# Tying each instruction to the one ahead of it on its engine, and placing every writer of a reused tile behind the old tile's readers

## The chip, the cores and the metric

One core of one Trainium2 chip. The metric is the device time of one execution in microseconds (us), on the slowest (here the only) core. "PE" is TensorE, "PEld" its weight load, "DVE" VectorE, "ACT" ScalarE, "POOL" GpSimd, "SP" SyncE. SBUF and PSUM are the on-chip memories that the kernel's tiles lie in (its matmuls write to banks of PSUM); a semaphore is a counter by which one engine waits for another. All timed runs below are of the fast state; in none did the granted TensorE clock averaged over the run fall under 0.988.

## The reference

Four graph layers on 128 graphs of 64 nodes with 256 features, each followed by a residual and a layer norm. Cut to what matters:

```python
x = layernorm(x + gated(x, adj))         # 5 rounds: message product, sum over neighbours, GRU cell
x = layernorm(x + mlp(adj @ x))          # 256 -> 1024, RMS norm, SiLU, 1024 -> 256
x = layernorm(x + hyperbolic(adj @ x))   # artanh (a logarithm), then tanh and a projection
x = layernorm(x + attention(x, adj))     # softmax-like weights by exp, masked by adj
```

## The kernel before

The graphs are worked on in 16 groups of 8. The kernel does not write its instructions straight out. It records every operation with an engine, an assumed duration, what it reads and what it writes; a beam search (one that carries several unfinished plans along and keeps the best) then simulates the engines and looks for an order in which PE never waits; the operations are emitted in the order found, which is called the plan below. Groups overlap, so that while one group waits for a small chain on DVE or ACT, PE works for another.

```python
    def op(self, eng, us, run, w=(), r=(), kb=0):          # record one operation
        ...
        for accesses, writes in ((r, False), (w, True)):
            for a in accesses:
                b, part = a if isinstance(a, tuple) else (a, None)
                if not b.uses and b.slot is not None:       # first use of a buffer in a reused slot:
                    ring = self.slots.setdefault(b.slot[0], deque(maxlen=b.slot[1]))
                    if len(ring) == b.slot[1]:
                        before.update(u[0] for u in ring[0].uses)   # behind all uses of the old one
                    ring.append(b)
        ...

    WINDOW, STRETCH, WIDTH, LAG = 4, 25.0, 8, 40.0          # groups looked at, us per decision, plans kept

    def issue(self):
        ...                                                 # the beam search
        for part in reversed(parts):
            for o in part:
                o.run()                                     # emit, in the plan's order
```

Below this lies a second scheduler, that of the framework. It takes the emitted instructions with their data dependencies, puts them in an order of its own on each engine, and adds the semaphores. Emission order is only a hint to it.

The operations that the argument comes back to:

```python
# a gated layer: copy of a partial product out of PSUM; the next product goes into the same bank after it
act(420, lambda: nc.scalar.copy(uu.tile(), blocks_of(p1.tile())), [uu], [p1])
...
# second layer: residual plus bias, added on GpSimd from two SBUF tiles
pool(2.35, lambda: nc.gpsimd.tensor_tensor(xb.tile(), x1.tile(), over(b2_r.tile(), NB), OP.add), [xb], [x1, b2_r])
...
# third layer: the logarithm of artanh, on ACT, with a table load before it and another after it
act(2600, lambda: nc.scalar.activation(fac.tile(), fac.tile(), AF.Ln), [fac], [fac])
...
# set-up: small vectors spread to all partitions by GpSimd's queue; sums over a_r on DVE into junk_d
a_r = everywhere(a_w, 2 * D, "a_r")
```

Of the kernel before, what the change touches and what calls it, by code (L numbers as in the profile page):

```python
# [14 lines left out]
OP = mybir.AluOpType  # L15
# [4 lines left out]
MIN_NORM = 1e-15  # L20
MAX_ARG = float(np.float32(1 - 1e-7))
MAX_NORM = 1.0 - 0.004
SERIES_BELOW = 0.25
# [3 lines left out]
class Buf:  # L27


    def __init__(self, make, slot=None, bank=False):  # L30
        self.make, self.slot, self.bank = make, slot, bank
        self.ap, self.uses, self.left = None, [], 0

    def __getitem__(self, i):
        return self.tile()[i]
# [15 lines left out]
class Plan:  # L51


    def __init__(self, flow):
# [4 lines left out]
        self.uses = {}  # L59
        self.clock = dict.fromkeys(flow.AHEAD, 0.75)  # L60
        self.queues = [{e: deque(o for o in s if o.eng == e) for e in self.clock} for s in flow.streams]
# [15 lines left out]
    def advance(self, until, rank):  # L77
# [3 lines left out]
        while self.left and clock["PE"] < until:  # L81
            best = None
            for s in range(self.first, min(self.first + flow.WINDOW, len(self.queues))):
                for e, q in self.queues[s].items():
                    opened = False
                    for _, o in zip(range(flow.AHEAD[e]), q):
                        t = max(clock[e], at[o.id])
# [53 lines left out]
class Flow:  # L141
# [7 lines left out]



    AHEAD = {"PE": 32, "DVE": 10, "ACT": 10, "POOL": 4, "SP": 2}

    HOPS = {"from PE": 0.25, "to PE": 0.3, "else": 0.1}
# [3 lines left out]
    TRANSFERS = 8  # L158
    WINDOW, STRETCH, WIDTH, LAG = 4, 25.0, 8, 40.0

    def __init__(self):
        self.streams, self.slots = [], {}

    def stream(self):
        self.ops = []
# [2 lines left out]
    def op(self, eng, us, run, w=(), r=(), kb=0):  # L168
        o = Op(eng, us, run, len(self.streams) - 1, len(self.ops), kb)
        before = set()  # L170
# [3 lines that stand above are left out]
                if not b.uses and b.slot is not None:  # L174
                    ring = self.slots.setdefault(b.slot[0], deque(maxlen=b.slot[1]))
                    if len(ring) == b.slot[1]:
                        before.update(u[0] for u in ring[0].uses)
                    ring.append(b)
                for u, p, wr in b.uses:
                    if (wr or writes) and (p is None or part is None or p == part):  # L180
                        before.add(u)
        before.discard(o)
        touched = set()
# [3 lines that stand above are left out]
                if b.bank and not b.uses:  # L187
                    o.opens = b
                b.uses.append((o, part, writes))
                if b not in touched:  # L190
                    touched.add(b)
                    b.left += 1
        o.bufs = [b for b in touched if b.bank]
        o.need = len(before)
        for u in before:
            u.then.append(o)
        self.ops.append(o)
# [18 lines left out]
    def issue(self):  # L216
        self.ways()
        ranks = (lambda s, o: (s, o.n), lambda s, o: (s if o.kb else -s, o.n), lambda s, o: (self.LAG * s - o.way, s, o.n))
        plans, until = [Plan(self)], 0.0
        while any(p.left for p in plans):  # L220
            until += self.STRETCH
            found = {}
            for p in plans:
                for rank in ranks:
                    c = p.copy()
                    if c.advance(until, rank):
                        found.setdefault((round(c.bound(), 3), c.left), c)
            plans = [found[k] for k in sorted(found)[:self.WIDTH]]
        p, parts = plans[0], []
        past = (p.past, p.order)  # L230
        while past is not None:
            parts.append(past[1])
            past = past[0]
        for part in reversed(parts):
            for o in part:
                o.run()


@with_exitstack
def kernel(  # L240
# [31 lines left out]
    nc = tc.nc  # L272
# [7 lines left out]
    KD = D // P  # L280
# [8 lines left out]
    small = ctx.enter_context(tc.tile_pool(name="small", bufs=2))  # L289
    psum = ctx.enter_context(tc.tile_pool(name="psum", bufs=BANKS, space=bass.MemoryType.PSUM))  # L290

    flow = Flow()
    quads = [slice(t * N, (t + 1) * N) for t in range(2)]


    def fixed(shape, name):
        return Buf(lambda: const.tile(shape, F32, name=name))
# [11 lines left out]


    def matmul(o, lhsT, rhs, k, nk):
        nc.tensor.matmul(o, lhsT, rhs, start=(k == 0), stop=(k == nk - 1))  # L312

    def pe(n, run, w, r):
        flow.op("PE", {512: 0.86, 256: 0.435, 257: 0.44, 128: 0.23}.get(n, 0.3), run, w, r)
# [4 lines left out]
    def dve(n, run, w, r):  # L320
        flow.op("DVE", 0.16 + 0.00105 * n, run, w, r)
# [44 lines left out]
    one4 = const.tile([P, NB], F32, name="one4")  # L366
# [28 lines left out]
    NV = 3 * KD  # L395
    NC = 2 * NV + 2 * KH
    cols = fixed([P, NC], "cols")
    half_b = fixed([P, NV], "half_b")
# [53 lines left out]


    def halves():
        nc.vector.tensor_add(half_b[:, :2 * KD], cols[:, :2 * KD], cols[:, NV:NV + 2 * KD])
        nc.vector.tensor_copy(half_b[:, 2 * KD:], cols[:, NV + 2 * KD:2 * NV])
        nc.vector.tensor_scalar(half_b.tile(), half_b.tile(), 0.5, None, OP.mult)
    dve(300, halves, [half_b], [cols])

    def turned(src, nf, out_of):  # L460
# [97 lines left out]
    def group(g):  # L558
        s = g % NF

        def tiny(name, shape=(P, NB), dt=F32):
            t = f"{name}{s}"
            return Buf(lambda: small.tile(list(shape), dt, tag=t, name=f"{name}_{g}"), slot=(t, 2))

        def u(tag, name, shape=(P, R)):
            return unit(tag, s, f"{name}_{g}", shape, bufs(tag))
# [27 lines left out]
        def aggregate(dst, src, b0, n):  # L594

            ps = bank("ps_agg")
            for j in range(2):
                for c in range(KD):
                    pe(128, lambda j=j, c=c: matmul(
                        ps[:, c * HR + j * P:c * HR + (j + 1) * P], src[:, b0 + j, c * P:(c + 1) * P],  # L600
                        ed[:, 2 * n + j, :], 0, 1), [ps], [(src, b0 + j), ed])
            act(512, lambda: nc.scalar.copy(dst[:, :, half(n)], blocks_of(ps.tile())), [(dst, n)], [ps])  # L602
            return ps
# [49 lines left out]
        for t in range(2):  # L653
            q = quads[t]
# [123 lines left out]
        for n in range(2):  # L778
            ps = rows_of(hT, n)
            for j in range(2):  # L780
                b = 2 * n + j
# [5 lines left out]
        for t in range(2):  # L787
            q = quads[t]
# [40 lines left out]
        for c in range(KH):  # L829
# [4 lines left out]
            th = u("VZR"[c % 3], f"th{c}")  # L834
# [5 lines left out]
        for h in range(NB // 2):  # L840
            ps = bank("ps_o1")
            for j in range(2):
                b = 2 * h + j
# [4 lines left out]
            for j in range(2):  # L848
                b = 2 * h + j
                dve(256, lambda ps=ps, b=b, j=j: nc.vector.scalar_tensor_tensor(  # L850
                    y1[:, b, :], ps[:, j * D:(j + 1) * D], 0.5, xb[:, b, :], OP.mult, OP.add), [(y1, b)], [ps, (xb, b)])
        xn = tiny("n")
# [3 lines left out]
        rn, fac, n2, ser = (tiny(t) for t in ("rn", "fac", "n2", "ser"))  # L856
        near = tiny("near", dt=I32)
# [9 lines left out]


        def series():
            nc.vector.tensor_mul(n2.tile(), xn.tile(), xn.tile())  # L870
            nc.vector.scalar_tensor_tensor(ser.tile(), n2.tile(), 1.0 / 13.0, one4, OP.mult, OP.mult)
            for q in (11, 9, 7, 5, 3):
                nc.vector.scalar_tensor_tensor(ser.tile(), ser.tile(), 1.0 / q, n2.tile(), OP.add, OP.mult)
            nc.vector.tensor_add(ser.tile(), ser.tile(), one4)
            nc.vector.scalar_tensor_tensor(near.tile(), xn.tile(), SERIES_BELOW, one4, OP.is_lt, OP.mult)
        dve(1250, series, [n2, ser, near], [xn])
        dve(4, lambda: nc.vector.scalar_tensor_tensor(fac.tile(), fac.tile(), 0.5, rn.tile(), OP.mult, OP.mult),
            [fac], [fac, rn])
# [7 lines left out]
        for h in range(NB // 2):  # L886
            for j in range(2):
                b = 2 * h + j
                pe(256, lambda b=b, j=j, ps=sup[h]: matmul(
                    ps[:, j * D:(j + 1) * D], adjT[:, b, :], tan[:, b, :], 0, 1), [sup[h]], [adjT, (tan, b)])  # L890
            for j in range(2):
                b = 2 * h + j
# [3 lines left out]
        un, unb, th, urn = tiny("n"), tiny("n2"), tiny("th"), tiny("rn")  # L896
# [3 lines left out]


        def onto_ball():
            nc.vector.tensor_mul(th.tile(), th.tile(), urn.tile())
            nc.vector.tensor_mul(un.tile(), th.tile(), un.tile())
            nc.vector.scalar_tensor_tensor(un.tile(), un.tile(), MIN_NORM, un.tile(), OP.max, OP.max)  # L905
            nc.vector.reciprocal(un.tile(), un.tile())
            nc.vector.scalar_tensor_tensor(un.tile(), un.tile(), MAX_NORM, one4, OP.mult, OP.min)
            nc.vector.tensor_mul(th.tile(), th.tile(), un.tile())
        dve(4, lambda: nc.vector.reciprocal(urn.tile(), unb.tile()), [urn], [unb])
        dve(800, onto_ball, [th, un], [th, un, urn])  # L910
        y2 = rows("y", "y2")
        for b in range(NB):
# [22 lines left out]
        for t in range(2):  # L935
            q = quads[t]
# [5 lines left out]
        for t in range(2):  # L942
            q = quads[t]
# [11 lines left out]
        o = layer_norm(y3, "A", "n3")  # L955
# [38 lines left out]
```

## Time and profile before

| | before |
|---|---|
| time, median of 4 | 2511.1 us (2510.5 to 2511.9) |
| span of the profiled run | 2509.0 us |
| PE busy / idle | 2438.9 / 70.1 us |
| DVE, ACT busy | 66%, 47% |
| sum of all PE instructions at their spacing | 2409 us |

The lines themselves are in the prediction. A row of the stretches gives start and end, the length, then for PE, PEld, DVE, ACT and POOL the busy time with the number of records, then granted clock, DMA share and GB/s. In a line of the timeline the first two numbers are start and duration; square brackets hold the engine's idle time just before, and what ended it.

One more measure is used throughout. PE's order of work is known from the program, and each PE instruction has a spacing when nothing holds it (0.432 us for 256 columns, and so on, as the prediction lists them). I add up these spacings along PE's order and call the running sum **PE work**, from 0 to 2409 us. A **gap** is what the distance between two starts has beyond the spacing. Gaps sorted by PE work can be compared between kernels of different length. For the kernel before: 10.1 us in the first 60 us of PE work (the start), 43.3 from 60 to 2100 (the middle), 3.9 from 2100 to 2330, and 30.6 beyond (the end).

### The profile page before, as it was taken

The numbers are of one execution on the slowest core, as the hardware profiler recorded it, in microseconds if no ns is written. First come the engines' busy times: TensorE is split into PE (matmuls) and PEld (weight loads), VectorE is DVE, ScalarE is ACT, GpSimd is POOL, SyncE is SP. The second block draws the span as 40 slices with busy tenths as digits, with TensorE's granted clock in tenths as the row PEclk, the third lists the DMA queues.
The fourth block names the chain that finished last, engine by engine and source line by source line (L and its number), as shares of the span: only waits on it lengthen the run. The fifth ranks groups of instructions, "written<-read, shape, count | busy, mean of one in ns | idle before, by whom it ended". The sixth has DMA issues, their size and how long they took to land. (4 is left out here: it accounts for less than half of the span.)

```text
span 2509.0 us, 31864 instructions
## 1 busy us (share of the span) xinstructions
PE 2438.9 (97%) x11986; PEld 2047.4 (82%) x11986; DVE 1659.8 (66%) x3725; ACT 1188.6 (47%) x2500; POOL 179.1 (7%) x146
## 2 busy tenths in 40 slices
PE   8999999999999999999999999999999999999995
PEld 6887887888787887887878878887888887878874
DVE  2656677667577676666776766676766665666766
ACT  3444445445445445445454454455445445444643
POOL 4001000000001000000010000010000000000011
PEclk9999999999999999999999999999999999999998
DMA  4000000000000000000000000000000000000000
GB/s 125 1 1 9 1 9 20 1 9 28 1 20 9 20 9 20 1 19 9 1 28 1 20 9 1 9 28 1 20 28 1 11 18 1 9 20 9 1 9 26
DMA packets 39146, 35.12 MB, mean 14 GB/s; under 512 B 9892, under 2 KB 38592, under 8 KB 38992
## 3 DMA queue, kind: packets, MB, share of 16 engines
q1 hardware_dynamic: 37264, 31.20, 3.9%
q8 instruction: 95, 1.56, 0.3%
q10 hardware_dynamic: 1328, 1.31, 0.2%
q0 software_dynamic: 400, 0.57, 0.1%
q14 instruction: 59, 0.48, 0.1%
HBM read 24.69 MB, written 8.39 MB: 13 GB/s over the span
## 5 line engine op out<-in xcount | busy, mean ns | idle before, releaser
L609 PE MATMUL p_hn<-hT,w_hn 128*128 128x256 f32 x1280 | 320.7, 380 | 0.0
L609 PE MATMUL p_in<-agg,w_in 128*128 128x256 f32 x1280 | 311.9, 379 | 0.0
L609 PEld LDWEIGHTS p_in<-agg,w_in 128*128 128x128 f32 x1280 | 241.3, 190 | 32.6 <-issue 1.0
L609 PEld LDWEIGHTS p_hn<-hT,w_hn 128*128 128x128 f32 x1280 | 229.0, 191 | 29.4 <-issue 4.8
L312 PE MATMUL ps_o<-w2s,hid 128*128 128x256 f32 x1024 | 234.0, 381 | 3.4 <-DVE n L905 3.0
L312 PE MATMUL ps_hid<-aggm,w1s 128*128 128x512 f32 x512 | 229.0, 592 | 0.0
L312 PEld LDWEIGHTS ps_o<-w2s,hid 128*128 128x128 f32 x1024 | 193.2, 191 | 30.2 <-issue 3.2
L624 POOL TENSOR_TENSOR rstd<-ve,pow 128x4 f32<-128x4 f32 (+1 forms) x64 | 77.5, 1211 | 1823.6 <-DVE ve L622 1823.5
L713 ACT ACTIVATE V<-V,half_b 128x256 f32<-128x256 f32 x160 | 72.8, 500 | 267.9 <-DVE V L709 267.9
L312 PEld LDWEIGHTS ps_hid<-aggm,w1s 128*128 128x128 f32 x512 | 95.3, 190 | 97.1 <-issue 92.4
L609 PE MATMUL p_r<-hT,a 128*128 128x256 f32 x640 | 155.1, 380 | 7.2 <-ACT U L739 5.9
L609 PE MATMUL p_u<-tA,s 128*128 128x256 f32 x640 | 157.3, 384 | 4.9 <-DVE tA L692 2.3
L609 PE MATMUL p_w<-tA,s 128*128 128x256 f32 x640 | 160.2, 380 | 1.7 <-DVE tA L692 1.7
L609 PE MATMUL p_r<-agg,a 128*128 128x256 f32 x640 | 153.4, 380 | 5.9 <-ACT agg L602 4.9
L609 PE MATMUL p_v<-tB,s 128*128 128x256 f32 x640 | 156.7, 379 | 0.0
L678 ACT ACTIVATE hnb<-p_hn,half_b 128x256 f32<-128x256 f32 x320 | 135.5, 471 | 44.6 <-PE p_hn L609 42.4
L609 PE MATMUL p_v<-tB,na 128*128 128x256 f32 x640 | 153.8, 380 | 2.1 <-DVE V L709 2.0
L722 DVE SCALAR_TENSOR_TENSOR R<-R,hnb 128x512 f32<-128x512 f32 x80 | 56.1, 701 | 150.1 <-ACT R L713 150.0
L609 PE MATMUL p_w<-hT,s 128*128 128x256 f32 x640 | 155.4, 379 | 0.0
L602 ACT COPY agg<-ps_agg 128x512 f32<-128x512 f32 x160 | 93.0, 583 | 119.2 <-PE ps_agg L312 94.4
L312 PEld LDWEIGHTS ps_agg<-edge,hr 128*128 128x128 f32 x1024 | 134.6, 191 | 11.3 <-ACT hr L672 4.9
L609 PEld LDWEIGHTS p_r<-hT,a 128*128 128x128 f32 x640 | 120.2, 190 | 28.4 <-ACT U L739 7.9
(206 smaller groups left out, 4447.1 us busy)
## 6 DMA issues: line engine op xcount, KB each, us to landing
x<-in_x_dram SPq DMA_DIRECT2D x16, 512.0 KB, 3.8
xr<-in_x_dram SPq DMA_DIRECT2D x16, 512.0 KB, 3.5
out_dram<-x_n SPq DMA_DIRECT2D x16, 512.0 KB, 2.8
edge<-in_adj_dram SPq DMA_DIRECT2D x32, 64.0 KB, 2.3
wm<-in_L_gnn_weight_dram SPq DMA_DIRECT2D x5, 256.0 KB, 7.3
w1s<-in_L_gnn_W_dram SPq DMA_DIRECT2D x1, 1024.0 KB, 6.8
w2s<-in_L_gnn_W_dram SPq DMA_DIRECT2D x1, 1024.0 KB, 9.6
aw_in_L_gnn_w_hh_dram<-in_L_gnn_w_hh_dram ACTq DMA_DIRECT2D x1, 512.0 KB, 5.3
```

What stands on the lines that cost most here:

```text
L312: nc.tensor.matmul(o, lhsT, rhs, start=(k == 0), stop=(k == nk - 1))
L602: act(512, lambda: nc.scalar.copy(dst[:, :, half(n)], blocks_of(ps.tile())), [(dst, n)], [ps])
L609: pe(256, lambda c=c, k=k: nc.tensor.matmul(ps[:, c * HR:(c + 1) * HR], w[:, k, c * P:(c + 1) * P], v(k), start=first and c == k == 0, sto ...
L624: pool(1.1, lambda: nc.gpsimd.tensor_tensor(rstd[:, :m, :], ve[:, :m, :], pow2[:, :m, :], OP.pow), [rstd], [ve])
L678: act(300, lambda c=c: nc.scalar.activation(hnb[:, c, half(n)], p_hn[:, c * HR:(c + 1) * HR], AF.Identity, bias=half_b[:, 2 * KD + c:2 * K ...
L713: act(256, lambda c=c: nc.scalar.activation(o[:, c, :], src(c), AF.Tanh, bias=half_b[:, i * KD + c:i * KD + c + 1], scale=0.5), [(o, c)], ...
L722: dve(512, lambda: nc.vector.scalar_tensor_tensor(t.tile(), t.tile(), 1.0, hnb[:, :, half(n)], OP.add, OP.mult), [t], [t, (hnb, (n, 0)), ( ...
```

## The change

Its intent: the search's order is to reach the chip. Every emitted instruction gets an ordering edge, without a semaphore, to the one emitted before it on its engine (the "ties"). And where a slot is reused, not the first writer alone but each writer is planned behind the old tile's uses (the "writers"). The helpers now return their instructions so that the ties can be drawn; those lines are cut.

```diff
@@ Flow
+    BEHIND = mybir.DependencyInfo(mybir.DependencyClass.NoSync, mybir.DependencyReason.DATA)
...
                     if len(ring) == b.slot[1]:
-                        before.update(u[0] for u in ring[0].uses)
+                        b.after = {u[0] for u in ring[0].uses}
                     ring.append(b)
+                if writes:
+                    before.update(b.after)
...
+        last = {}
         for part in reversed(parts):
             for o in part:
-                o.run()
+                made = o.run()
+                for i in made if isinstance(made, list) else [made]:
+                    if o.eng in last:
+                        self.tc.add_manual_dep(i.ins, last[o.eng].ins.name, self.BEHIND, reason="the plan's order")
+                    last[o.eng] = i
```

More of the change, by code (lines that the diff above doesn't have):

```diff
@@ L31, in __init__ @@
         self.make, self.slot, self.bank = make, slot, bank
-        self.ap, self.uses, self.left = None, [], 0
+        self.ap, self.uses, self.left, self.after = None, [], 0, ()
     def __getitem__(self, i):
@@ L159, with __init__ @@
     WINDOW, STRETCH, WIDTH, LAG = 4, 25.0, 8, 40.0
-    def __init__(self):
-        self.streams, self.slots = [], {}
+    BEHIND = mybir.DependencyInfo(mybir.DependencyClass.NoSync, mybir.DependencyReason.DATA)
+    def __init__(self, tc):
+        self.tc, self.streams, self.slots = tc, [], {}
     def stream(self):
@@ L290 @@
     psum = ctx.enter_context(tc.tile_pool(name="psum", bufs=BANKS, space=bass.MemoryType.PSUM))
-    flow = Flow()
+    flow = Flow(tc)
     quads = [slice(t * N, (t + 1) * N) for t in range(2)]
@@ L311, in matmul @@
     def matmul(o, lhsT, rhs, k, nk):
-        nc.tensor.matmul(o, lhsT, rhs, start=(k == 0), stop=(k == nk - 1))
+        return nc.tensor.matmul(o, lhsT, rhs, start=(k == 0), stop=(k == nk - 1))
     def pe(n, run, w, r):
@@ L454, in halves @@
     def halves():
-        nc.vector.tensor_add(half_b[:, :2 * KD], cols[:, :2 * KD], cols[:, NV:NV + 2 * KD])
-        nc.vector.tensor_copy(half_b[:, 2 * KD:], cols[:, NV + 2 * KD:2 * NV])
-        nc.vector.tensor_scalar(half_b.tile(), half_b.tile(), 0.5, None, OP.mult)
+        return [nc.vector.tensor_add(half_b[:, :2 * KD], cols[:, :2 * KD], cols[:, NV:NV + 2 * KD]),
+                nc.vector.tensor_copy(half_b[:, 2 * KD:], cols[:, NV + 2 * KD:2 * NV]),
+                nc.vector.tensor_scalar(half_b.tile(), half_b.tile(), 0.5, None, OP.mult)]
     dve(300, halves, [half_b], [cols])
@@ L869, in series @@
         def series():
-            nc.vector.tensor_mul(n2.tile(), xn.tile(), xn.tile())
-            nc.vector.scalar_tensor_tensor(ser.tile(), n2.tile(), 1.0 / 13.0, one4, OP.mult, OP.mult)
-            for q in (11, 9, 7, 5, 3):
-                nc.vector.scalar_tensor_tensor(ser.tile(), ser.tile(), 1.0 / q, n2.tile(), OP.add, OP.mult)
-            nc.vector.tensor_add(ser.tile(), ser.tile(), one4)
-            nc.vector.scalar_tensor_tensor(near.tile(), xn.tile(), SERIES_BELOW, one4, OP.is_lt, OP.mult)
+            v = nc.vector
+            return [
+                v.tensor_mul(n2.tile(), xn.tile(), xn.tile()),
+                v.scalar_tensor_tensor(ser.tile(), n2.tile(), 1.0 / 13.0, one4, OP.mult, OP.mult),
+                *(v.scalar_tensor_tensor(ser.tile(), ser.tile(), 1.0 / q, n2.tile(), OP.add, OP.mult)
+                  for q in (11, 9, 7, 5, 3)),
+                v.tensor_add(ser.tile(), ser.tile(), one4),
+                v.scalar_tensor_tensor(near.tile(), xn.tile(), SERIES_BELOW, one4, OP.is_lt, OP.mult)]
         dve(1250, series, [n2, ser, near], [xn])
@@ L902, in onto_ball @@
         def onto_ball():
-            nc.vector.tensor_mul(th.tile(), th.tile(), urn.tile())
-            nc.vector.tensor_mul(un.tile(), th.tile(), un.tile())
-            nc.vector.scalar_tensor_tensor(un.tile(), un.tile(), MIN_NORM, un.tile(), OP.max, OP.max)
-            nc.vector.reciprocal(un.tile(), un.tile())
-            nc.vector.scalar_tensor_tensor(un.tile(), un.tile(), MAX_NORM, one4, OP.mult, OP.min)
-            nc.vector.tensor_mul(th.tile(), th.tile(), un.tile())
+            v = nc.vector
+            return [
+                v.tensor_mul(th.tile(), th.tile(), urn.tile()),
+                v.tensor_mul(un.tile(), th.tile(), un.tile()),
+                v.scalar_tensor_tensor(un.tile(), un.tile(), MIN_NORM, un.tile(), OP.max, OP.max),
+                v.reciprocal(un.tile(), un.tile()),
+                v.scalar_tensor_tensor(un.tile(), un.tile(), MAX_NORM, one4, OP.mult, OP.min),
+                v.tensor_mul(th.tile(), th.tile(), un.tile())]
         dve(4, lambda: nc.vector.reciprocal(urn.tile(), unb.tile()), [urn], [unb])
```

## The prediction

> **What bounds the kernel now.** I read first the busy times of the engines, then the table of stretches, then the list of waits, and last single moments in order of time. The head of the page:
>
> ```profile
> span 2509.0 us, 31864 instructions
> ## 1 busy us (share of the span) xinstructions
> PE 2438.9 (97%) x11986; PEld 2047.4 (82%) x11986; DVE 1659.8 (66%) x3725; ACT 1188.6 (47%) x2500; POOL 179.1 (7%) x146
> ```
>
> TensorE (PE) is the bound: it is idle for 2509.0 - 2438.9 = 70.1 us, while VectorE (DVE) has 850 us to spare and ScalarE (ACT) more. The change neither adds nor removes a matmul, so only PE's idle time can move. Where it lies, from the stretches (after the stretch's length: PE busy with its number of records, then PEld, DVE, ACT, POOL, clock, DMA):
>
> ```profile
> 0.00:62.00 62.00, 54.95 (x245) 41.96 (x246) 16.29 (x47) 20.46 (x50) 25.73 (x34) 0.94 0.41 126
> ...
> 125.00:600.00 475.00, 470.21 (x2332) 397.38 (x2331) 311.97 (x635) 230.09 (x481) 22.95 (x17) 1.00 0.03 10
> 600.00:1200.00 600.00, 588.93 (x2916) 496.34 (x2915) 404.50 (x907) 289.19 (x609) 37.35 (x28) 1.00 0.04 11
> 1200.00:1800.00 600.00, 591.09 (x2920) 498.13 (x2919) 410.40 (x952) 290.67 (x612) 41.05 (x30) 1.00 0.04 12
> 1800.00:2300.00 500.00, 494.50 (x2462) 418.05 (x2461) 337.32 (x716) 237.91 (x502) 27.39 (x20) 1.00 0.04 12
> 2300.00:2440.00 140.00, 136.89 (x633) 108.28 (x632) 93.47 (x227) 70.98 (x142) 13.39 (x9) 1.00 0.01 5
> 2440.00:2509.00 69.00, 39.36 (x168) 31.32 (x166) 47.44 (x180) 23.20 (x49) 9.76 (x9) 0.86 0.07 23
> ```
>
> Length minus PE busy: 7.1 us at the start, 0 + 4.8 + 11.1 + 8.9 + 5.5 + 3.1 = 33.4 us in the long middle (62 to 125 has none), and 29.6 us in the last 69 us, where no other group of rows is left to fill PE. These three parts answer to different causes. The list of waits names those of the middle (us in total, times, longest):
>
> ```profile
> PE p_r L609 <- ACT U L739: 5.9, 5, 1.7
> PE p_r L609 <- ACT agg L602: 4.9, 5, 1.4
> PE p_u L609 <- DVE tA L692: 2.3, 4, 1.0
> PE p_u L609 <- DVE ser L871: 2.2, 1, 2.2
> PE p_v L609 <- DVE V L709: 2.0, 3, 1.4
> ```
>
> They are few and short, with matmuls of the gated layers waiting for a copy or a sum that another engine was late with. Why late? At one of them:
>
> ```profile
> 1387.68 1.28 ACT L866 ACT_TABLE_LOAD   x1
> 1388.41 0.16 DVE L874 TENSOR_TENSOR ser<-ser,one 128x4 f32<-128x4 f32 x1
> 1388.98 0.20 ACT L866 ACTIVATE fac<-fac 128x4 f32<-128x4 f32 x1
> 1389.09 0.57 ACT L739 COPY U<-p_r 128x512 f32<-128x512 f32 x1
> ...
> 1389.71 0.48 PE L609 MATMUL p_r<-hT,a 128*128 128x256 f32 x1 [1.73 <-ACT U L739]
> ```
>
> The kernel's own search put the copy of `U` ahead of the logarithm `fac` (the copy carries creation number 9066, the logarithm 9070), but the emitted ACT queue has them the other way round. The logarithm and its table load, 1.28 + 0.20 = 1.48 us, went first, and PE stood still for 1.73 us. The same pair, in the same wrong order, precedes the waits at 762 and 1540 us.
>
> **What the Trainium skill says.** "PSUM — Partial Sum Buffer", section "Engine vs sequencer instructions", states that the ACT, DVE and GpSimd queues are strict FIFO and that matmuls start in program order. The trace agrees: every one of the 3719 DVE and 2439 ACT records I matched stands where the emitted program has it, and the copy above waits behind a logarithm of another group. So the emitted order is the order that runs. "Perfetto Trace Analysis", section "Identifying the Most-Contended Engine", says that matmul busy time is a poor measure of closeness to the roofline. That holds here: the ends are modelled, so short gaps hide in "busy". I therefore also use spacing. Back-to-back 256-column matmuls start 0.432 us apart (four in 1.727 us), 512-column ones 0.859, 128-column ones 0.223, transposes 0.11; summed over all 6570 PE instructions of the program this makes 2409 us. The span is thus 100 us above a PE that never waits. Of these, gaps between starts hold 88: 10.2 before 62 us, 47.7 from 62 to 2415, and 30.6 after; the other 12 lie before the first matmul, after the last, and in rounding. Finally, the same page's "Identifying Dependency Chains" says that extra wait instructions may be put in where one instruction waits for several engines. The built programs have them: 362 on PE before and 389 after, DVE 567 and 525, ACT 337 and 343. One that is already satisfied took 17 ns on ACT in this trace; 27 more on PE is under half a microsecond, as an estimate.
>
> **The change, part by part.** (1) *The ties.* Each instruction gets an ordering edge, without a semaphore, to the one the plan issued before it on its engine. No work is added. Creation numbers show what it moves: in the program before, 207 of 6570 PE instructions, 1771 of 3719 on DVE and 495 of 2406 on ACT stand behind one that was created later; after, none on these three. DVE, where nearly half had been overtaken, changes most. (2) *The writers.* Before, only the first writer of a reused buffer was planned behind the old buffer's readers; now each is. The semaphores were already right, so this changes only the plan: the two plans agree for the first 1442 PE instructions (514 us of PE work) and differ afterwards. It makes the plan more truthful, which matters more now that it is obeyed.
>
> What part (1) is worth: I matched each PE gap to the result that ended it, and looked whether, in the 6 us before, a later-created instruction ran ahead of that result on its engine. This is so for 6.1 + 12.7 + 10.8 + 8.8 = 38.4 of the 47.7 us in the middle (stretches to 600, 1200, 1800, 2415). The overtakers take 0.6 to 3.5 us in the larger cases, the size of the gaps. But presence isn't proof: with half of DVE overtaken, some stand there by chance, and some gaps would only shrink. I choose 70%: 38.4 x 0.7 = 27 us. At the start, 3.3 us of waiting for `edge` have two overtakers of 0.85 us together: 1 us. In the tail PE waits 9.7 us for `x_n` of the last group, on a chain of dependent small operations; overtakers there total 1.3 us; with the smaller tail waits I take 1.5 us. Against this, new waits where the plan's assumed durations are wrong and the queue now can't slide around them: I choose 2 us, as the assumptions are near the trace (256-column matmul 0.435 against 0.432; 512-wide DVE operation 0.70 against 0.70). Sum: 27 + 1 + 1.5 - 2 = 27.5 us less. From 2511.1 that is **2483 us**, 1.1% less.
>
> **Rivals.** (a) *All middle gaps close.* That the plan's durations are near the trace's speaks for it; the 9.3 us without any overtaker speak against. It would save 47.7 + 3 = 51 us: 2460 us, just beyond 2%. (b) *The order is stiff.* The reordering that is now forbidden also let ready work fill holes; with ties one late DMA or logarithm holds the whole queue. For it: the plan gives the logarithm 2.27 us, where the trace has 1.28 + 0.20 + 1.28 with the return load. Against: groups overlap, with PE work queued from several, and DVE is a third idle. It would give back the saving: 2505 to 2520 us. (c) *The altered plan ends worse.* The tail is 30 us, the largest single piece. But summed PE work puts the last group's last gated layer at 2351 us before and 2353 after, and its first wide hidden product at 2362 and 2357: the same 56 to 58 us of work remain behind the last layer. I expect +/-3 us. (d) *DVE becomes the bound.* No: its work is unchanged at 66%, and its waits on itself fall from 1888 to 1695 as counted in the programs.
>
> **Range and chances.** The low end takes about 90% of the middle and 2 us of tail (2466); the high end takes 27% of the 38.4 and nothing else (2501). Over 2% faster needs 50 us, all of the middle and more: 5%. Over 2% slower would need rival (b) beyond anything seen: 1.5%.
>
> **What the changed profile would show.** PE idle between 62 and 2440 us down from 33.4 to about 12 to 16; waits of `p_r` for ACT `U` and `agg` nearly gone; no table load directly ahead of a copy of `U` that PE is waiting for; PE busy lower by some microseconds as hidden gaps close; the last 69 us again with about 28 us idle; DVE and ACT busy unchanged within 1%. I am wrong if the middle's idle stays above 28 us, or if the tail moves by more than 5 us: then the plan, and not the emission, was at fault.

## The result

The changed kernel takes 2478.45 us (median of 4, 2477.4 to 2480.7) against 2511.09. The ratio of fast runs is 0.9871, with a 95% interval of 0.9854 to 0.9888: 1.3% faster, clear of noise but under 2%. A ratio here is the mean time of one kernel's fast runs over that of the other's in the same rounds, so it is not quite the ratio of the medians.

The head of the changed kernel's page (its line numbers are 10 to 14 higher than before, for the added lines):

```profile
span 2478.9 us, 31858 instructions
...
PE 2430.3 (98%) x11986; PEld 2052.0 (83%) x11986; DVE 1714.4 (69%) x3725; ACT 1197.1 (48%) x2500; POOL 179.7 (7%) x146
```

PE is idle for 48.6 us in place of 70.1, and 8.6 us of short gaps have left its "busy" as well. The stretches of the changed kernel, cut at the same times except that the last is again the last 69 us:

```profile
0.00:62.00 62.00, 58.88 (x278) 44.85 (x279) 20.30 (x49) 22.82 (x56) 27.17 (x34) 1.00 0.41 126
...
125.00:600.00 475.00, 474.94 (x2372) 404.53 (x2371) 323.29 (x639) 232.51 (x485) 23.15 (x17) 1.00 0.03 9
600.00:1200.00 600.00, 598.39 (x2975) 508.19 (x2974) 432.64 (x973) 297.39 (x624) 41.91 (x31) 1.00 0.04 13
1200.00:1800.00 600.00, 599.50 (x2984) 509.21 (x2983) 427.24 (x925) 297.13 (x622) 37.72 (x28) 1.00 0.04 11
1800.00:2300.00 500.00, 497.48 (x2446) 417.83 (x2445) 350.12 (x728) 249.51 (x510) 32.58 (x22) 0.99 0.04 12
2300.00:2410.00 110.00, 98.73 (x455) 80.41 (x454) 67.40 (x165) 50.09 (x107) 9.51 (x7) 0.94 0.02 6
2410.00:2479.00 69.00, 39.40 (x161) 30.84 (x159) 52.90 (x178) 20.13 (x39) 7.66 (x7) 0.84 0.07 23
```

Length minus PE busy: 3.1 us at the start, 0.1 + 1.6 + 0.5 + 2.5 to 2300 us, then 11.3 in the 110 us that follow, and 29.6 in the last 69. The long middle has hardly any idle time left; but the end now begins earlier, and it is longer. The longest of PE's waits say the same:

```profile
PE ps_T L589 <- DVE x_n L648: 6.1, 1, 6.1
PE ps_hr L599 <- DVE hT L744: 5.6, 3, 3.5
PE ps_agg L322 <- DVE x_n L648: 5.1, 1, 5.1
```

Waits of `p_r` for ACT are gone from the list. `ps_T` waited at the end before, too:

```profile
PE ps_T L579 <- DVE x_n L638: 10.3, 2, 9.7
```

`ps_hr` and `ps_agg` are mostly new, at 2375 and 2381 us. One of the places where a copy of `U` meets a logarithm in the changed kernel:

```profile
911.47 0.56 ACT L749 COPY U<-p_r 128x512 f32<-128x512 f32 x1
912.05 1.28 ACT L876 ACT_TABLE_LOAD   x1
912.23 1.89 PE L619 MATMUL p_r<-hT,a 128*128 128x256 f32 x8
```

The copy goes first, the product follows without a wait, and the table load runs beside it.

The gaps by PE work, for all kernels of this study (us; the experiments' names are explained below):

| kernel | start, to 60 | middle, 60 to 2100 | 2100 to 2330 | end | ratio to before |
|---|---|---|---|---|---|
| before | 10.1 | 43.3 | 3.9 | 30.6 | 1 |
| changed | 3.1 | 4.0 | 6.7 | 41.6 | 0.9871 |
| writers_only | 11.4 | 33.9 | 9.4 | 40.9 | 1.0022 |
| tie_dve | 8.3 | 18.8 | 7.6 | 43.6 | 0.9959 |
| tie_act | 11.6 | 22.6 | 6.7 | 39.9 | 0.9977 |
| tie_dve_act | 8.0 | 4.0 | 5.2 | 41.8 | 0.9884 |
| tie_dve_pool | 3.0 | 18.7 | 5.9 | 42.7 | 0.9929 |
| wide | 3.0 | 6.0 | 0.5 | 30.9 | 0.9797 |
| lag25 | 5.5 | 17.0 | 0.1 | 28.8 | 0.9847 |
| wide20 | 3.4 | 7.1 | 0.0 | 28.3 | 0.9787 |
| xb_memset | 3.3 | 1.2 | 1.7 | 38.3 | 0.9829 |
| xb_dve_best | 3.6 | 1.8 | 0.0 | 26.2 | 0.9773 |

So the change is -7.0 us at the start, -39.3 in the middle, +2.8 and +11.0 towards the end: -32.5. The span fell by 30.1; the other 2.4 us are nearly all the time after PE's last start, 9.8 us before and 12.0 after.

### The profile page after: what moved, and what is told of

Its sections match the earlier page's. It is cut to its first block, busy times and chain, and to the rows that moved or that the text cites. A ratio compares the mean times of both kernels' runs of the same rounds, so it can differ in the third digit from the quotient of the medians.

```text
span 2478.9 us, 31858 instructions
## 1 busy us (share of the span) xinstructions
PE 2430.3 (98%) x11986; PEld 2052.0 (83%) x11986; DVE 1714.4 (69%) x3725; ACT 1197.1 (48%) x2500; POOL 179.7 (7%) x146
## 4 chain that ended last, share of the span: by engine, by line
PE 96%; DVE 2%; ACT 1%; DMA 0%; issue 0%; POOL 0%; ACTq 0%; DVEq 0%; POOLq 0%
PE p_w L619 11%; PE p_v L619 11%; PE p_hn L619 11%; PE p_r L619 11%; PE p_in L619 11%; PE ps_hid L322 9%; PE ps_o L322 9%; PE ps_agg L322 7%; PE p_u L619 6%; PE ps_hr L599 3%; PE ps_a L322 2%; PE ps_T L589 1%; PE ps_sup L322 1%; PE ps_wmih L322 1%; PE ps_att L322 1%; PE ps_ss L322 0%
## 5 line engine op out<-in xcount | busy, mean ns | idle before, releaser
L322 PEld LDWEIGHTS ps_o<-w2s,hid 128*128 128x128 f32 x1024 | 192.6, 190 | 30.6 <-DVE hid L847 5.3
L723 ACT ACTIVATE R<-p_r,half_b 128x256 f32<-128x256 f32 x160 | 68.0, 472 | 148.0 <-PE p_r L619 147.4
L322 PE MATMUL ps_agg<-edge,hr 128*128 128x128 f32 x1024 | 138.5, 275 | 0.0
```

The source lines that it names most:

```text
L322: return nc.tensor.matmul(o, lhsT, rhs, start=(k == 0), stop=(k == nk - 1))
L723: act(256, lambda c=c: nc.scalar.activation(o[:, c, :], src(c), AF.Tanh, bias=half_b[:, i * KD + c:i * KD + c + 1], scale=0.5), [(o, c)], ...
```

## The experiments

Two questions: which part of the change did what, and why the end grew. Each edit is against the changed kernel.

**The ties without the writers.** This was meant to be the first run, and it can't be one: the build ends with

```
DOES NOT BUILD: DeadlockException: Deadlock detected!
```

The old plan lets a second writer of a reused tile go ahead of the old tile's readers (if it is run again, it has two such writers, both on ACT), which the semaphores forbid. With a free order the framework sorts that out; with the order nailed down it can't. The two parts of the change are therefore not independent: the second makes the first possible.

**The writers without the ties** (`writers_only`):

```diff
-                    if o.eng in last:
+                    if False and o.eng in last:
```

> The changed kernel's plan, with every ordering edge left out: the emission is free to reorder again. Theory T (the broken order makes the middle's waits; the writers' part only changes the plan, and makes its end worse): gaps between PE starts from 60 to 2100 us of PE work stay at 35 to 50 us (before 43.3, after 4.0), the end beyond 2330 us of PE work at 32 to 44 (before 30.6, after 41.6), the time 2510 to 2530 us. Rival R (it is the more truthful plan that closes the gaps, and the ties are a formality): middle below 15 us, time 2475 to 2490 us.

Measured: ratio 1.0022 (1.0015 to 1.0029), 2519.7 us. The stretch from 62 to 2200 us in the kernel before, in this run and in the changed kernel:

```profile
62.00:2200.00 2138.00, 2107.74 (x10456) 1783.65 (x10455) 1430.89 (x3128) 1024.96 (x2162) 124.37 (x91) 1.00 0.03 11
```
```profile
62.00:2200.00 2138.00, 2118.63 (x10513) 1793.36 (x10512) 1429.69 (x3087) 1031.73 (x2165) 119.14 (x89) 1.00 0.03 11
```
```profile
62.00:2200.00 2138.00, 2135.83 (x10642) 1816.96 (x10641) 1499.60 (x3181) 1052.12 (x2201) 126.29 (x92) 1.00 0.04 11
```

PE is idle there for 30.3, 19.4 and 2.2 us. The new plan alone takes something from the middle (33.9 us of gaps in place of 43.3, just under the expected range), but loses as much at the end, where its gaps are already the changed kernel's: 40.9 against 41.6. Theory T holds: the ties empty the middle, and the longer end comes with the plan. From 1.0022 to 0.9871 the ties are worth 1.5%, some 38 us.

**Ties on one engine** (`tie_dve`, and `tie_act` with ACT in its place):

```diff
-                    if o.eng in last:
+                    if o.eng in last and o.eng in ('DVE',):
```

> The changed kernel with the ties on DVE alone. Theory T-DVE (DVE, where nearly half of the instructions had been overtaken, is what makes PE wait, ACT's lateness being mostly handed on from it): middle gaps (60 to 2100 us of PE work) 5 to 15 us, time 2480 to 2490 us. Theory T-both (ACT's own disorder counts as much; in the kernel before, 22 us of the overtaken middle gaps ended with an ACT result and 16 with a DVE one): middle 15 to 28 us, time 2490 to 2505 us.

> The changed kernel with the ties on ACT alone. Theory T-DVE: middle gaps stay at 30 to 42 us, time 2505 to 2525 us. Theory T-both: middle 15 to 26 us, time 2490 to 2505 us, about as much as ties on DVE alone give.

Measured: 2505.0 us (0.9959) and 2509.6 us (0.9977). The middle keeps 18.8 us of gaps with DVE tied and 22.6 with ACT tied, of 33.9 with neither. Both of these lie in the range of "both", though DVE counts for a little more. The times do not separate the theories: 2505.0 is at the upper end of "both", and 2509.6 is 4.6 us over it and inside the range of the rival. The expectation had left out that the start stayed long (8.3 and 11.6 us, where the changed kernel has 3.1); the reading rests on the gaps.

**Ties on both** (`tie_dve_act`): the same edit with `('DVE', 'ACT')`.

> The changed kernel with ties on DVE and ACT, while PE, the GpSimd queue and SyncE stay free. Theory S (the middle's waits come from the disorder of DVE and ACT together, which the ties on either alone only half removed: 18.8 and 22.6 us left of 33.9): middle gaps (60 to 2100 us of PE work) 3 to 9 us; the start stays at 7 to 11 us, because its loads are still issued in the wrong order from the GpSimd queue; time 2483 to 2493 us. Rival P (PE's own 64 overtaken matmuls hold the rest): middle 12 to 20 us, time 2493 to 2503 us.

Measured: 2485.3 us (0.9884), middle 4.0 us, as in the changed kernel. So DVE's and ACT's order together are the whole of the middle. PE's own order, which here has 64 matmuls still overtaken, adds nothing that shows. What is left to the changed kernel is the start: 8.0 against 3.1 us.

**The start** (`tie_dve_pool`). In the kernel before, this happens on DVE and PE:

```profile
14.59 0.42 DVE L554 SCALAR_TENSOR_TENSOR junk_d<-wb_r,a_r 128x256 f32<-128x256 f32 x1 [4.89 <-DMA a_r<-in_L_gnn_a_w_dram]
...
16.75 1.62 PE L312 MATMUL ps_agg<-edge,x 128*128 128x128 f32 x6 [3.16 <-DVE edge L655]
```

A set-up sum into `junk_d`, wanted only at the fourth layer, had been moved ahead of `edge`, which PE needs at once. The sum takes 0.42 us; but DVE stood 4.89 us for its load. The load itself was early too: GpSimd's queue had five broadcast loads issued from 4.5 us on, which the plan has later. With DVE alone tied, the sum no longer blocks, yet the first weights `wm` still land late. So I tied `('DVE', 'POOL')`.

> The changed kernel with ties on DVE and on the GpSimd queue. In the profiles where that queue is free, five broadcast loads (640 KB written) are issued between 4.5 and 8.7 us, ahead of their turn, and the first layer weights land in 7.3 to 8.0 us from issue; in the changed kernel these loads come later and the weights land in 4.6 us. Theory L (those loads share the 16 DMA engines with the weights and make them late): start gaps fall from 8.3 us with DVE alone to 3 to 4.5, weights land in 4.3 to 5.5 us, the rest as with DVE alone (middle 15 to 22), time 4 to 6 us under that run's 2505. Rival M (the start is set by something else, such as PE's or ACT's order there): start 7 to 9 us, time within 2 us of 2505.

Measured: 2496.5 us, 0.9929 against 0.9959 for DVE alone. The landing of `wm` (last number, us from issue) with DVE tied, and with DVE and GpSimd tied:

```profile
wm<-in_L_gnn_weight_dram SPq DMA_DIRECT2D x5, 256.0 KB, 8.0
```
```profile
wm<-in_L_gnn_weight_dram SPq DMA_DIRECT2D x5, 256.0 KB, 4.8
```

The start's gaps fall from 8.3 to 3.0 us. Theory L holds on both numbers. (In the expectation, 640 KB should be 513: by the traces the five loads are 128, 128, 256 and twice 0.5 KB; and with the queue free the weights took up to 8.4 us, in `writers_only`.) By the medians the time fell by 8.5 us, by the ratios by 7.5, where 4 to 6 were expected; each of the two ratios is known to about 4 us, so the excess is not clear of noise. In the two profiles the gaps fell by 5.3 us at the start, and by 2.6 beyond 2100 us of PE work, for which I have no cause. The Trainium skill, "Trainium Kernel Development and Optimization", section "Key Constraints", says that transfers issued from the different queues all run on the same 16 DMA engines and interleave; a load issued out of turn on one queue delaying loads on another agrees with that.

**Is the longer end a price of the writers?** (`wide`) Every plan comes with its own reckoning of PE's idle time. For the kernel before it has none in the middle and 31.1 us at the end; for the changed kernel 2.2 us at 2100 to 2330 and 36.3 at the end. A wider beam:

```diff
-    WINDOW, STRETCH, WIDTH, LAG = 4, 25.0, 8, 40.0
+    WINDOW, STRETCH, WIDTH, LAG = 4, 25.0, 48, 40.0
```

> The changed kernel with the beam of its search widened from 8 to 48 plans; nothing else differs. The plan it picks has by its own reckoning 31 us of PE idle at the end and nothing in the middle, against 36 at the end and 2 before it. Theory E (with the order kept, the chip follows the plan, so what the plan loses at the end is lost on the chip and can be bought back by a better plan): end gaps beyond 2330 us of PE work fall from 41.6 to 30 to 35 us, those from 2100 to 2330 from 6.7 to under 3, the middle stays under 8, time 2464 to 2472 us. Rival F (the longer end is the price of the strict order itself, whatever the plan): end gaps stay at 38 to 45 us and the time within 4 us of the changed kernel's 2478.

Measured: 2464.2 us (0.9797, interval 0.9781 to 0.9814), end 30.9, 2100 to 2330 0.5, middle 6.0. All in the ranges of theory E. The end's length is not inherent in the true constraints or in the ties; with 8 plans kept, the search had let the better endings go.

**Does the chip follow a worse plan, too?** (`lag25`) The same line with `4, 25.0, 8, 25.0`, whose plan has idle stretches in known places.

> The changed kernel with one constant of the search, the lag between groups, at 25 in place of 40. Its plan is worse by its own reckoning: PE idle 10.8 us at 600 to 1200 us of PE work, 5.6 at 1800 to 2100, 0.6 at 2250 to 2330 and 30.4 at the end (the changed kernel's plan: 0, 0, 0, 36.3). Theory E (with ties the chip does what the plan says, stretch by stretch): gaps of 10 to 15 us at 600 to 1200, 5 to 9 at 1800 to 2100, under 3 in each of the other middle stretches, 29 to 34 at the end; time 2482 to 2492 us. Rival N (the chip's own durations blur the plan, the stretches don't answer to it): no stretch stands out in the middle, or the end stays near 41.

Measured: 7.8 us at 600 to 1200 and 6.0 at 1800 to 2100, against 2.4 and 0.8 in the other two middle stretches; end 28.8, just under its range; 2475.4 us (0.9847). The waits stand where the plan has them, but smaller than expected in the first stretch, and the time is 7 us below the range. By its own reckoning this plan ends 11 us after the changed kernel's, and yet it ran no slower: 0.2% faster by the ratios, though the intervals (0.9832 to 0.9861, and 0.9854 to 0.9888) just overlap. So a plan is a good map of the places; its total is no reliable ranking, and the changed kernel's end had something that its plan did not know.

**A better ending** (`wide20`): `4, 20.0, 48, 40.0`.

> The changed kernel with a beam of 48 plans and decisions every 20 us in place of 25. Its plan has 26.9 us of PE idle at the end and none in the middle (the beam of 48 at 25 us: 31.1, and 30.9 on the chip). Theory E: end gaps 26 to 30 us, middle under 8, start 3; time 2458 to 2463 us, over 2% faster than the kernel before. Rival F2 (what the profile shows at the end is a floor of dependent small operations, near 31 us): end 30 to 34, time 2463 to 2468 us.

Measured: 2461.4 us (0.9787), end 28.3, middle 7.1. Theory E, against a floor near 31. Whether it is over 2% faster, as expected, stays unclear: the interval is 0.9771 to 0.9804.

**What the plan did not know** (`xb_memset`). I set the changed kernel's plan beside its trace, instruction by instruction. They run in step, PE gaining a steady 1% on the plan, but for 1.8 us at 694 us and 0.6 at 1381, until 2206 us, where one DVE addition takes four times its usual 0.69 us:

```profile
2205.72 2.35 POOL L809 TENSOR_TENSOR xb<-x_n,b_r 128x1024 f32<-128x1024 f32 x1 [2.66 <-ACT x_n L644]
2205.80 2.82 DVE L827 TENSOR_TENSOR sqs<-sqs,sq 128x512 f32<-128x512 f32 x1
...
2209.01 0.32 PE L946 MATMUL ps_e<-ident,ho 128*128 128x128 f32 x1 [0.61 <-DVE ho L942]
```

It ends 0.55 us after GpSimd's addition, which is not quite its own usual length. Nine DVE instructions over 1.5 us long stand in this trace, all with two SBUF inputs and all beside one of the 16 `xb` additions; two, at 691 and 1379 us, stand ahead of the losses at 694 and 1381, and a second one near the end (2383 us) lies in the chain that PE waits for at 2387. The Trainium skill, "SBUF — State Buffer", section "Who interferes with whom", says that a DVE instruction with two SBUF inputs contends with a GpSimd instruction that reads SBUF, and not with one that only writes it. To test just that, with the same order on PE, DVE and ACT:

```diff
-        pool(2.35, lambda: nc.gpsimd.tensor_tensor(xb.tile(), x1.tile(), over(b2_r.tile(), NB), OP.add), [xb], [x1, b2_r])
+        pool(2.35, lambda: nc.gpsimd.memset(xb.tile(), 0.0), [xb], [x1, b2_r])
```

> The changed kernel, same plan and same order on PE, DVE and ACT, but GpSimd's 16 additions into xb (2.35 us each, reading SBUF) are replaced by a memset of xb, which only writes. The result is wrong on purpose: the residual is lost. In the changed kernel nine DVE instructions with two SBUF inputs took 1.5 to 2.8 us in place of 0.16 to 0.69, all nine while an xb addition ran, two of them near the end (2206 and 2383 us); the gaps beyond 2100 us of PE work were 48.3 us, 9.8 more than the plan has. Theory G (those held DVE instructions make the chip's end longer than the plan's): no DVE instruction over 1.5 us, gaps at 2100 to 2330 us of PE work 0 to 3.5 (was 6.7), at the end 34 to 39 (was 41.6), time 2465 to 2473 us. Rival H (the held instructions lie beside other waits, the end is long for another reason): end 40 to 43 us, time 2474 to 2479 us.

Measured: 2469.9 us (0.9829); the result is wrong, as intended. No DVE instruction over 1.5 us is left. Gaps at 2100 to 2330 fall from 6.7 to 1.7 us, at the end from 41.6 to 38.3, in the middle from 4.0 to 1.2. Theory G holds. The memset is also shorter (0.95 us against 2.35), so it could seem that it merely leaves less time to be held in. The trace answers this: it starts at the same point of the work (it still waits for `x_n`), and the addition on DVE begins as soon after it as before, but now takes its usual time:

```profile
2203.03 0.95 POOL L809 MEMSET xb<- 128x1024 f32 x1 [2.64 <-ACT x_n L644]
2203.13 0.68 DVE L827 TENSOR_TENSOR sqs<-sqs,sq 128x512 f32<-128x512 f32 x1
```

The same is so of the instructions at 369, 691, 1585 and 2383 us, which began 0.07 to 0.5 us after an addition and took 2.3 to 2.7 us: beside the memset, as early, they took 0.17 to 0.69. In the changed kernel, eleven DVE instructions that began during an addition had both inputs in SBUF and were held (the nine, and two of 1.11 us; one more, which began 0.06 us before an addition's end, was not), while eleven with one input in PSUM kept their usual length. The held instructions of `wide` and `wide20`, ten over 1.5 us in each, agree: the last of them stand at 1818 and 2159 us, and neither kernel's end is much longer than its plan's.

**A version that beats both** (`xb_dve_best`), with the right result: `xb` is added on DVE, which the search can plan, and the search runs with `3, 20.0, 48, 40.0` (that line of the edit is cut). Several things change at once, so this run does not separate their shares.

```diff
-        pool(2.35, lambda: nc.gpsimd.tensor_tensor(xb.tile(), x1.tile(), over(b2_r.tile(), NB), OP.add), [xb], [x1, b2_r])
+        dve(1024, lambda: nc.vector.tensor_tensor(xb.tile(), x1.tile(), over(b2_r.tile(), NB), OP.add), [xb], [x1, b2_r])
```

> A version meant to beat both kernels, with right results: ties and writers kept, xb added on DVE (planned at 1.24 us) and not on GpSimd, the search with 48 plans, decisions every 20 us and a window of 3 groups. Its plan has 26.6 us of PE idle at the end and none in the middle, the same as the beam of 48 at 20 us with xb on GpSimd (26.9), which ran 2461 us. Theory G: without held DVE instructions the chip keeps to the plan or under it, end gaps 23 to 28 us, middle under 4, time 2453 to 2459 us. Rival H2 (16 more DVE operations cost what the held ones did): middle 6 to 10, time 2459 to 2465 us.

Measured: 2456.2 us, ratio 0.9773 (0.9758 to 0.9787), faster by over 2%. Middle 1.8 us, end 26.2. PE is 99% busy:

```profile
PE 2422.7 (99%) x11986; PEld 2046.9 (83%) x11986; DVE 1719.1 (70%) x3741; ACT 1198.1 (49%) x2500; POOL 141.5 (6%) x130
```

## Why the prediction was right, and where its steps failed

The total was right: 2483 predicted, 2478 measured. The bound, the direction and the mechanism (an operation late because a later one had been put ahead of it) are confirmed by `writers_only` and `tie_dve_act`. But of its four terms three were mis-sized, and one of these had the wrong sign. The middle gave 39.3 us where 27 less 2 were forecast, the start 7.0 where it was 1, and beyond 2100 us of PE work 13.8 us were lost where 1.5 were to be gained. That such errors leave the total within 5 us is luck.

- **"38.4 x 0.7 = 27 us" in the middle.** Too small. From 60 to 2330 us of PE work the gaps fell from 47.2 to 10.7 us, by 36.5, though 2.8 of this came back late; up to 2100 us 39.3 of 43.3 went. The term was reckoned for the ties alone, and set against `writers_only` they took 29.9 us (33.9 to 4.0), not far from 27. The other 9.4 us (43.3 to 33.9) went with the new plan while the order was still free; to the plan the prediction had given nothing, and why it helped there is not shown. So the runs do not say that the discount of 70%, for overtakers that stood there by chance, was wrong. Rival (a), that all middle gaps close, was nearly right about the middle.
- **"At the start ... 1 us."** It was 7.0. I counted the overtakers' own 0.85 us. What an overtaker costs is its own time plus its *wait*: DVE stood 4.89 us for the load of `a_r`. And I compared the order on PE, DVE and ACT only; GpSimd's queue, whose loads made the weights late, was the larger part: the start's gaps are 11.4 us with no ties, 8.3 with DVE's and 3.0 with DVE's and GpSimd's.
- **"1.5 us for the tail", and rival (c) at +/-3 us.** The end grew by 11.0 us, with 2.8 more just before it. I compared where PE's *work* stands, which hardly moved, and took the tail for unchanged. That view can't see how long the DVE and ACT chains are in between. `writers_only` shows that the new plan brings the longer end with it, and `wide` that a better search does without it; `xb_memset` shows 8.3 us of the last two stretches' 48.3 to come with GpSimd's additions. The prediction's own sign for failure ("if the tail moves by more than 5 us") was met. Its forecast for the profile hid this: the last 69 us do have 29.6 us idle, near the forecast 28, but the end now begins before them. PE's idle time between 62 and 2440 us fell to 23.4 us and not to 12 to 16; up to the last 69 us it is 16.0.
- **"Less 2" for new waits in the middle.** There was room for this in the middle: 4.0 us in all are left there, 2.8 of which went with `xb_memset`. Stiffness, rival (b), did not show.
- **"DVE and ACT busy unchanged within 1%."** Wrong for DVE, 1659.8 to 1714.4 us (3.3%). The instructions' durations add up to 1855.5 and 1869.8 us, some 5 us of the difference being held instructions; but in the free order 2443 of them start before the one ahead has ended, and in the plan's order 1884. Rival (d) still doesn't hold: PE is the bound.
- **Order and waits.** That the emitted order is the order that runs, and that extra wait instructions on PE (389 against 362) cost nothing visible, agrees with the two kernels' programs and traces. The estimate of "under half a microsecond" took ACT's 17 ns for one, though; 360 of PE's own 362 took 51 ns in the trace before, which would make 1.4 us. And 9066 and 9070 are the numbers of the tiles `U` and `fac`; the instructions are 9067 and 9087, in the same order.

Open: what separates the 38.3 us that remain at the end in `xb_memset` from its plan's 36.3, why `lag25` ran faster than its plan by more than the others did, and the 2.6 us by which `tie_dve_pool` gained beyond its start.

## What to carry to other kernels

If a kernel searches for its own instruction order, check on the emitted program that it survives the layer below; here nearly half of DVE's instructions had been overtaken, and the disorder cost 1.5% of a kernel that was 97% busy on its bound. Once the order is kept, the plan is what runs: the dependencies it leaves out can become deadlocks, its ending shows in the kernel's ending, and contention that it does not model (GpSimd and DVE on SBUF) becomes visible. In weighing an overtaker, count its wait for its own inputs and not only its duration, and look at every queue that issues transfers.

## What the Trainium skill lacked or had wrong

- "SBUF — State Buffer", "Who interferes with whom", is confirmed for DVE instructions with two SBUF inputs, and the runs add a size: beside a GpSimd addition of 2.35 to 2.68 us, DVE instructions that usually take 0.16 to 0.69 us took 1.5 to 2.8 us in nine of the changed kernel's 16 cases, and none did beside a memset. (One TENSOR_SCALAR with a single SBUF input took 0.86 us in place of 0.41 beside a memset, at 2375 us of `xb_memset`.)
- "Perfetto Trace Analysis", "Identifying the Most-Contended Engine", calls occupancy a fair measure of how close VectorE is to roofline. It depends on the order as well: the same instructions were busy 1659.8 us in one order and 1714.4 in another. Their durations account for 14.3 us of the difference (1855.5 against 1869.8 in sum); the other 40 us are overlap of neighbours that one order has and the other has not.
- "Perfetto Trace Analysis", "Optimization Strategy", says to find the gaps and the instruction that ends them, and to make it start sooner. It lacks the question whether that instruction was late because another stood ahead of it in its queue: putting this right was worth some 38 us here. I found no page on what a difference between written and emitted order costs in time.
